# Tap loads of a Fourier convolution: 68 transfers of one tap each in place of 20 transfers of one row group each

## The chip, the cores and the metric

The kernel runs on one core of a Trainium2 chip. The metric is the device time of one execution in microseconds. Three runs of the kernel before are known, and one more execution that was recorded by the hardware profiler.

## What is computed

The input `x` holds 128 graphs of 128 nodes with 256 channels in f32, and `adj` a 128x128 matrix for each graph. Two layers follow one another, each of the form `x = x + layer(relu(layernorm(x)))`. The change touches only the second convolution of the first layer, so that part is shown and the rest is named:

```
h  = relu(bn1(conv1x1(xc)))                  # xc: 256 channels x 128 nodes
h  = bn2(conv1d(h, conv2_w, 17 taps, pad 8))
x_conv = relu(h + xc)
A  = exp(-pairwise squared distance) * adj ; x_nmp = A @ relu(x @ w_msg + b_msg)
out = GRU gates from [x_conv, x_nmp] and x
```

The second layer is a sum of five small graph convolutions over the first 25 nodes of each graph.

## The kernel before, in words

The convolution with 17 taps is done in the Fourier domain. 80 real frequency coefficients are used, and for each of them a 256x256 weight matrix is needed. These matrices are made on the chip from `conv2_w`, whose layout in memory is [256 input channels, 17 taps, 256 output channels].

*Tap weights* (`load_taps`, lines 426 to 433, and `tap_weights`, lines 435 to 474). The 256 input channels are worked off in four groups `n` of 64. One group is loaded into a tile `wt` of 128 partitions x 16 x 256. The 64 channels are four row groups `r` of 16 channels: partitions 32r to 32r+16 hold the 17 taps of row group `r`, and along the free axis lie its 16 channels with 256 outputs each. Two `wt` tiles exist, so group `n+2` can be loaded only when TensorE has read all of group `n`. For each of eight steps `m` TensorE multiplies the 17 rows of each row group by the 17x80 matrix `tap` (four matmuls `pw`, line 450), ScalarE and VectorE copy the four results into a tile `ws` (lines 455 and 457), and after every second step GpSimd issues four stores of 320 KB from `ws` to the tensor `wfd` in memory (line 462). There are two `ws` tiles: the copies of step `m` wait until the stores of step `m-4` have landed. In all 64 stores write 20 MB.

*Stage A* (`stage_a`, lines 367 to 418) runs beside it. For each group `q` of four graphs it loads `xa` with four transfers of 128 KB on SyncE (line 359; four `xa` tiles), takes the layernorm statistics on VectorE (`st`, `mv`, line 267 on), raises the variance to the power -1/2 on GpSimd (`rs`, line 270), normalizes on VectorE (line 275), transposes on TensorE (`ph`, line 386), writes `hTa` by a ReLU on ScalarE (line 388), stores it from GpSimd (`hTd`, line 391), multiplies by `c1w` (`pc`, line 397), adds a row on VectorE (`h`, line 400), and transforms to 80 coefficients (`pf`, line 408) that are copied into `X`. The first 16 of the 32 groups come in the first pass.

*After it*, `early` (line 632) computes the neighbour part of graph groups from reloaded `hT`, and `stage_b` (line 477) multiplies `X` by the weights reloaded from `wfd`. Then the second half of stage A and stage B, and the rest of both layers.

*Order.* Each engine executes its instructions in the order in which the program issues them. That order is written by a small planner (`Lane`, `Order`, lines 156 to 204): each part of the work is a generator whose `yield cost, delay` tells how much TensorE time it has just issued and after how much planned time it may go on. The planner alternates between the lanes by their planned times and weights. The lane `beside` holds `tap_weights` and then `early(0)`, `early(1)` and so on. The first `yield` of `tap_weights`, line 437, sets when the lane starts: after 16 planned microseconds.

*Queues.* Transfers are issued by SyncE, ScalarE and GpSimd, and each of these issues in order: a transfer that has to wait holds up what is behind it. In the compiled program the transfers of SyncE and ScalarE share eight completion semaphores, which are handed out in turn, and those of GpSimd have eight of their own. A transfer that gets a semaphore whose earlier transfer hasn't landed waits for it. Before the tap loads of group 0, ScalarE issues `cst`, `vec` and `c1w`, and SyncE `xa0` and `xa1`. Behind them GpSimd has the powers of `fold` (lines 286 and 270) and ScalarE its first ReLU.

Group 0 of the taps is loaded by the call at line 1103 on three queues. Groups 1, 2 and 3 are loaded from inside `tap_weights` on SyncE and GpSimd (line 441): group 1 at step 3 of group 0, and the others at step 0 of the group before. Behind GpSimd's part stand further `rs` powers, `hTd` stores and `wfd` stores.

Of the kernel before, what the change touches and what calls it, by code (L numbers as in the profile page):

```python
# [16 lines left out]
TAPS, PAD = 17, 8  # L17
# [190 lines left out]
def kernel(ctx: ExitStack, tc: tile.TileContext, x, adj, consts, vecs, w_se, conv1_w,  # L208
                    conv2_w, w_msg, b_msg, w_ih, w_hh, W1, W2, b2, fusion_w, out):
    nc = tc.nc  # L210
# [22 lines left out]
    def c(name):  # L233
        a, b = CAT[name]
        return cst[:, a:b]
# [14 lines left out]
    def load_late():  # L250

        nc.sync.dma_start(out=wse, in_=w_se.rearrange("(k p) o -> p k o", p=P))
        nc.sync.dma_start(out=cst[:, CFIRST:], in_=consts[:, CFIRST:])
# [73 lines left out]
    def fold_embedding():  # L327

        nc.vector.memset(wse9, 0.0)
        for role in range(3):  # L330
            nc.vector.tensor_copy(wse9[:, :, 3 * role:3 * role + 3], wse[:, :, :3])
        pbs = ptmp.tile([P, 512], FP, tag="tmp", name="pbs")
        nc.tensor.matmul(pbs[:, :1], c("sel"), v("b_se"), start=True, stop=True)
        bse = cp.tile([P, 1], FP, name="bse")
        nc.vector.tensor_copy(bse, pbs[:, :1])
        nc.vector.scalar_tensor_tensor(embb, emb[:, 4:8], bse, emb[:, 8:12],
                                       op0=ALU.mult, op1=ALU.add)
        yield 1.5, 0.0
# [23 lines left out]
    def load_xa(q):  # L362
        if q not in XA:
            XA[q] = LATE["ab"].tile([P, 4, D], FP, tag="xa", name=f"xa{q}", bufs=4)
            load_x(XA[q], q)
# [60 lines left out]
    def load_taps(n, *engines):  # L426

        wt = tw.tile([P, 16, D], FP, tag="wt", name=f"wt{n}")
        src = conv2_w.rearrange("(r n i) t o -> n t r i o", r=4, n=4)[n]
        for r in range(4):  # L430
            engines[r % len(engines)].dma_start(out=wt[32 * r:32 * r + 16], in_=src[:16, r])
        engines[0].dma_start(out=wt[16::32], in_=src[16])
        wts.append(wt)

    def tap_weights():

        yield 0.0, 16.0
        for n in range(4):
            for m in range(8):
                if m == (0 if n else 3) and n < 3:  # L440
                    load_taps(n + 1, nc.sync, nc.gpsimd)
                if (n, m) == (1, 3):
                    load_late()
                if m % 2 == 0:
                    ws = tw.tile([P, 4, 4, D], FP, tag="ws", name=f"ws{n}_{m}")
                pws = [(pgat if r < 3 else ptmp).tile([P, 2, D], FP, tag="gat" if r < 3 else "tmp",
                                                      name=f"pw{n}_{m}_{r}") for r in range(4)]
                for r in range(4):
                    rows = slice(32 * r, 32 * r + TAPS)
                    nc.tensor.matmul(pws[r][:F], c("tap")[rows], wts[n][rows, 2 * m:2 * m + 2],  # L450
                                     start=True, stop=True)
                i = m % 2 * 2
                for r in range(4):
                    if r < 2 or (r == 2 and m % 2):
                        nc.scalar.activation(ws[:F, r, i:i + 2], pws[r][:F], AF.Copy)
                    else:
                        nc.vector.tensor_copy(ws[:F, r, i:i + 2], pws[r][:F])
                yield 0.9, 2.2
                if m % 2:
                    for r in range(4):  # L460
                        i0 = 64 * r + 16 * n + 2 * (m - 1)
                        nc.gpsimd.dma_start(out=wfd[:, i0:i0 + 4], in_=ws[:F, r])
        yield from fold_embedding()
        mid.close()
        wg = ctx.enter_context(tc.tile_pool(name="wg", bufs=1, reuse_waits="tile"))
        LATE["wrz"] = wg.tile([P, 7, 3, D], FP, name="wrz")
        LATE["wn"] = wg.tile([P, 7, 2, P], FP, name="wn")
        LATE["wh"] = wg.tile([P, 7, 1, P], FP, name="wh")
        LATE["io"] = near.enter_context(tc.tile_pool(name="io", bufs=2, reuse_waits="tile"))
        LATE["fr"] = near.enter_context(tc.tile_pool(name="fr", bufs=1, reuse_waits="tile"))  # L470
        LATE["wmsg"] = LATE["fr"].tile([P, 2, D], FP, name="wmsg")
        LATE["bmsg"] = LATE["fr"].tile([P, D], FP, name="bmsg")
        nc.sync.dma_start(out=LATE["wmsg"], in_=w_msg.rearrange("(k p) o -> p k o", p=P))
        nc.sync.dma_start(out=LATE["bmsg"], in_=b_msg.partition_broadcast(P))
# [625 lines left out]
    load_xa(0)  # L1100
    nc.scalar.dma_start(out=c1w, in_=conv1_w.rearrange("(k p) o -> p k o", p=P))
    load_xa(1)
    load_taps(0, nc.sync, nc.gpsimd, nc.scalar)
    load_xa(2)
    fold()
    beside = Lane([tap_weights()] + [early(q) for q in range(NQ)])
    gates = Lane([fold_gates()], weight=0.5)
    for bat, (during_a, during_b) in enumerate(((0.66, 0.5), (0.2, 0.65))):
# [60 lines left out]
```

## Time and profile before

| | |
|---|---|
| three runs | 2124.36, 2126.18, 2129.80 us |
| median of the runs | 2126.18 us |
| the profiled execution's own time | 2123.29 us |
| its span, first to last instruction | 2121.2 us |
| mean granted TensorE clock | 0.989 |
| moved by DMA | 281.66 MB, mean 133 GB/s |

The share of busy time on the page is a mean over stages that differ: up to about 212 us the tap weights and stage A run, to about 630 us the first products and the second pass of stage A, and after 700 us the gates and the second layer, in which the DMA engines are busy 30% of the time on the mean. The page's 40 slices are 53 us each:

```
PE   6998999999999999999999999999999999999998
DMA  9997778744787534233223232323222332323121
```

A digit is the busy share of a slice in tenths. In the first three slices DMA and TensorE are both near full. Arrows in a timeline name what ended the idle time before an instruction; "issue" means that the profile shows no waiting. DMA engines are not told apart in the views; a "share" of over 1 comes from packets that overlap on an engine.

### The profile page before, as it was taken

How to read it: one execution, taken by the hardware profiler on the slowest of the kernel's cores; microseconds unless marked ns; L12 is line 12 of the kernel's file. 1: busy time of each engine (PE TensorE's matmuls, PEld its weight loads, DVE VectorE, ACT ScalarE, POOL GpSimd, SP SyncE). 2: the span in 40 equal slices, each digit the busy share in tenths (PEclk: the TensorE clock that was granted, in tenths of full speed). 3: DMA queues.
4: the chain of work that ended last, by engine and by line, in shares of the span. 5: the costliest groups of instructions: out<-in, count | busy, mean ns of one | idle time of the engine just before them, and what ended most of it. 6: DMA issues, size and time to landing. Idle time of an engine off the chain costs nothing.

```text
span 2121.2 us, 30965 instructions
## 1 busy us (share of the span) xinstructions
PE 2056.6 (97%) x11316; PEld 1656.3 (78%) x11316; DVE 1177.2 (55%) x2775; ACT 687.6 (32%) x1543; POOL 723.2 (34%) x900
## 2 busy tenths in 40 slices
PE   6998999999999999999999999999999999999998
PEld 5566888789888787787778777878787787778775
DVE  5665444786544455645654654566455555654542
ACT  3554222344222233332232332232233323223233
POOL 2442666231565123422332233233213323233230
PEclk9999999999999999999999999999999999999999
DMA  9997778744787534233223232323222332323121
GB/s 182 264 269 231 242 267 261 213 145 150 254 267 253 184 110 153 61 100 77 73 71 83 84 83 71 107 73 78 80 82 75 83 97 75 78 80 102 36 68 50
DMA packets 187050, 281.66 MB, mean 133 GB/s; under 512 B 20685, under 2 KB 140242, under 8 KB 186898
## 3 DMA queue, kind: packets, MB, share of 16 engines
q1 hardware_dynamic: 156066, 184.81, 31.2%
q0 software_dynamic: 30000, 94.13, 13.7%
q8 instruction: 90, 1.47, 0.3%
q10 hardware_dynamic: 832, 0.74, 0.2%
q14 instruction: 62, 0.51, 0.1%
HBM read 187.34 MB, written 92.27 MB: 132 GB/s over the span
## 4 chain that ended last, share of the span: by engine, by line
PE 88%; DVE 3%; DMA 3%; POOL 2%; ACT 2%; issue 1%; SPq 0%; POOLq 0%; DVEq 0%; ACTq 0%
PE p L708 39%; PE pa L501 7%; PE pm L600 5%; PE ph L1029 5%; PE pz L1038 5%; PE pc L397 4%; PE pb L501 3%; PE pf L408 3%; PE px L626 3%; PE pi L673 2%; PE pg L1072 1%; DMA wfd<-ws 1%; PE po L853 1%; PE ph L386 1%; PE pw L450 1%
## 5 line engine op out<-in xcount | busy, mean ns | idle before, releaser
L833 POOL TENSOR_TENSOR d<-hTc,r 128x512 f32<-128x512 f32 x64 | 81.4, 1272 | 371.1 <-ACT r L830 371.1
L501 PE MATMUL pa<-wf,X 128*128 128x256 f32 x640 | 152.4, 381 | 0.0
L862 POOL DMA_DIRECT2D out<-xt x128 | 71.8, 566 | 204.2 <-DVE xt L859 201.5
L723 ACT ACTIVATE z<-z,brz 128x256 f32<-128x256 f32 x128 | 58.1, 501 | 253.3 <-DVE z L778 205.6
L524 DVE SCALAR_TENSOR_TENSOR y<-pa,kk 128x512 f32<-128x512 f32 x78 | 53.8, 690 | 147.4 <-ACT kk L523 147.4
L708 PE MATMUL p<-th,wrz 128*128 128x256 f32 x512 | 131.8, 380 | 0.0
L708 PE MATMUL p<-tc,wrz 128*128 128x256 f32 x512 | 131.6, 379 | 0.0
L708 PE MATMUL p<-tm,wrz 128*128 128x256 f32 x512 | 131.4, 379 | 0.0
L501 PEld LDWEIGHTS pa<-wf,X 128*128 128x128 f32 x640 | 118.1, 190 | 16.4 <-issue 2.2
L397 PE MATMUL pc<-c1w,hTa 128*128 128x256 f32 x512 | 124.4, 389 | 3.5 <-ACT ef L588 2.3
L600 PE MATMUL pm<-wmsg,hT 128*128 128x256 f32 x512 | 124.0, 388 | 0.0
L690 DVE SCALAR_TENSOR_TENSOR xc<-pc,s_bn,hTc 128x256 f32<-128x256 f32 x128 | 53.1, 477 | 117.3 <-PE pc L687 117.3
L708 PE MATMUL p<-hTc,wrz 128*128 128x256 f32 x384 | 106.1, 399 | 10.1 <-ACT u L742 10.1
L397 PEld LDWEIGHTS pc<-c1w,hTa 128*128 128x128 f32 x512 | 95.3, 194 | 22.2 <-DVE h L400 4.0
L1029 PE MATMUL ph<-yz,w 128*128 128x96 f32 (+3 forms) x640 | 111.5, 329 | 0.9 <-DVE yz L1014 0.9
L708 PEld LDWEIGHTS p<-hTc,wrz 128*128 128x128 f32 x384 | 68.3, 191 | 55.6 <-ACT u L742 22.5
L600 PEld LDWEIGHTS pm<-wmsg,hT 128*128 128x128 f32 x512 | 97.4, 193 | 16.7 <-issue 1.6
L1031 ACT ACTIVATE hh<-ph,vec 128x96 f32<-128x96 f32 (+3 forms) x160 | 64.3, 403 | 139.8 <-PE ph L1029 130.9
L1038 PE MATMUL pz<-hh,w 128*128 128x96 f32 (+3 forms) x640 | 107.7, 322 | 0.0
L708 PEld LDWEIGHTS p<-tm,wrz 128*128 128x128 f32 x512 | 97.3, 190 | 13.2
L1029 PEld LDWEIGHTS ph<-yz,w 128*128 128x128 f32 x640 | 90.1, 197 | 21.8 <-issue 15.5
L708 PEld LDWEIGHTS p<-th,wrz 128*128 128x128 f32 x512 | 94.5, 190 | 12.6 <-issue 0.6
(203 smaller groups left out, 4590.4 us busy)
## 6 DMA issues: line engine op xcount, KB each, us to landing
wf<-wfd SPq DMA_DIRECT2D x160, 256.0 KB, 3.9
wfd<-ws POOLq DMA_DIRECT2D x64, 320.0 KB, 7.3
yd<-y POOLq DMA_DIRECT2D x80, 256.0 KB, 3.7
yt<-yd SPq DMA_DIRECT2D x64, 320.0 KB, 4.9
w<-in_W SPq DMA_DIRECT2D x40, 512.0 KB, 3.6
xa<-in_x SPq DMA_DIRECT2D x128, 128.0 KB, 5.0
hTd<-hTa POOLq DMA_DIRECT2D x32, 512.0 KB, 5.0
hT<-hTd SPq DMA_DIRECT2D x32, 512.0 KB
```

The source lines that it names most:

```text
L397: nc.tensor.matmul(pc[:, i], hT[:, k, (2 * h + i) * N:(2 * h + i + 1) * N], c1w[:, k], start=(k == 0), stop=(k == 1))
L408: nc.tensor.matmul(pf[:, i, :F * NB], h1[:, 2 * h + i, k * P:(k + 1) * P], fwd, start=True, stop=True)
L501: nc.tensor.matmul(ps, xk(k), WF[f][:, k, s], start=(k == 0), stop=(k == 1))
L600: nc.tensor.matmul(pm[:, i], hT[:, k, j * N:(j + 1) * N], LATE["wmsg"][:, k], start=(k == 0), stop=(k == 1))
L626: nc.tensor.matmul(px[:, dc, i], msgs[h][:, i, dc * P:(dc + 1) * P], aT[:, 2 * h + i], start=True, stop=True)
L708: nc.tensor.matmul(ps[:, m], w[:, i, k, m * P:(m + 1) * P], factor(i, x, t), start=first and j == 0, stop=last and j == len(n) - 1, skip_g ...
L723: nc.scalar.activation(dst[:, m], src[:, m], AF.Sigmoid, bias=brz[:, b + m:b + m + 1])
L833: nc.gpsimd.tensor_sub(d, hT[:, dc], r[:, dc])
L862: nc.gpsimd.dma_start(out=out[q * GB + j, WIDE:].rearrange("(t n) c -> n t c", n=WIDE), in_=xt[j * WIDE:(j + 1) * WIDE, 1:4])
L1029: nc.tensor.matmul(ph, w1[:, k, m * P:(m + 1) * P], yz[:, k, :, o:o + n], start=(k == 0), stop=(k == 1))
L1031: nc.scalar.activation(hh[:, m], ph, AF.Relu, bias=v("b1", g * 4 + m))
L1038: nc.tensor.matmul(pz, w2[:, g, m, cc * P:(cc + 1) * P], hs[g][:, m], start=(m == 0), stop=(m == 3))
```

## The change

Three places differ. In `load_taps` the five transfers of a group (four of 16 taps x 16 channels, 256 KB each, into 16 neighbouring partitions, and one of 64 KB for the 17th tap into partitions 16, 48, 80 and 112) become 17 transfers of 64 KB: transfer `t` takes tap `t` of all 64 channels into partitions t, 32+t, 64+t and 96+t. They go alternately to two queues, the first of which gets nine. For group 0 the queues are GpSimd and ScalarE, no longer SyncE, GpSimd and ScalarE; for the other groups they stay SyncE and GpSimd. And the lane of the tap weights starts after 12 planned microseconds instead of 16.

```diff
         wt = tw.tile([P, 16, D], FP, tag="wt", name=f"wt{n}")
         src = conv2_w.rearrange("(r n i) t o -> n t r i o", r=4, n=4)[n]
-        for r in range(4):
-            engines[r % len(engines)].dma_start(out=wt[32 * r:32 * r + 16], in_=src[:16, r])
-        engines[0].dma_start(out=wt[16::32], in_=src[16])
+        for t in range(TAPS):
+            engines[t % len(engines)].dma_start(out=wt[t::32], in_=src[t])
         wts.append(wt)
 
     def tap_weights():
 
-        yield 0.0, 16.0
+        yield 0.0, 12.0
@@
     load_xa(1)
-    load_taps(0, nc.sync, nc.gpsimd, nc.scalar)
+    load_taps(0, nc.gpsimd, nc.scalar)
     load_xa(2)
```

In the compiled order the number of instructions on TensorE and VectorE stays as it is. From the first `pw` on, the tap work stands about one group of four matmuls and a half tile of stage A further ahead on every engine, and the interleaving of the two lanes stays shifted until well after the first products. SyncE's order becomes `xa0` to `xa4`, nine taps of group 1, `xa5`, `xa6`, nine of group 2, `xa7`, two constants, `xa8` to `xa10`, nine of group 3, `xa11` and so on. Before it was `xa0`, `xa1`, three transfers of group 0, `xa2` to `xa5`, three of group 1, `xa6`, `xa7`, three of group 2, `xa8` and so on.

## The prediction

> **What bounds the kernel now.** I read the page first, then busy time by stretch, the chain of waits from 60 to 200 us, the timelines of the first 36 us, and last the DMA view of single stretches.
>
> ```profile
> span 2121.2 us, 30965 instructions
> PE 2056.6 (97%) x11316; PEld 1656.3 (78%) x11316; DVE 1177.2 (55%) x2775; ACT 687.6 (32%) x1543; POOL 723.2 (34%) x900
> wt<-in_conv_w SPq DMA_DIRECT2D x8, 256.0 KB, 6.5
> wt<-in_conv_w POOLq DMA_DIRECT2D x7, 256.0 KB, 12.2
> ```
>
> TensorE is the bound, 97% busy. The change adds no TensorE work, so it can only move TensorE's 64.6 us of idle time and the stretches at half clock that follow idle time. The tap loads run in the first 130 us, so I looked for loss up to 212 us.
>
> ```profile
> 0.00:36.00 36.00, 18.11 (x84) 15.15 (x88) 16.86 (x63) 6.82 (x12) 6.10 (x11) 0.95 0.96 165
> 36.00:78.00 42.00, 42.00 (x263) 28.48 (x256) 29.82 (x78) 26.34 (x56) 19.28 (x29) 1.00 0.95 233
> 78.00:84.00 6.00, 0.77 (x4) 0.36 (x3) 0.84 (x2) 0.86 (x2) 1.53 (x3) 1.00 1.09 267
> 84.00:113.00 29.00, 29.00 (x159) 18.81 (x158) 21.98 (x59) 16.61 (x36) 13.48 (x20) 0.88 0.93 278
> 172.00:188.00 16.00, 12.05 (x82) 9.63 (x80) 8.26 (x27) 6.95 (x15) 5.44 (x7) 0.95 0.82 246
> ```
>
> The columns after the stretch are its length, busy time of PE, PEld, DVE, ACT and POOL, then granted clock, DMA share and GB/s. The reader is to see one hole, 78 to 84 us, and that the 29 us after it ran at 0.88 of the clock: 5.2 us idle plus 29 x 0.12 = 3.4 us slow, 8.6 us together. Its cause is in the chain:
>
> ```profile
> 68.85 0.90 POOL wfd L462
> 71.68 11.35 DMA wfd<-ws
> 83.14 0.60 ACT ws L455
> 83.78 2.49 PE pw L450 x8
> ```
>
> The second columns are durations. ACT may not fill the next `ws` until GpSimd's store of an earlier one has landed, and that store took 11.35 us where the page's median is 7.3. What the DMA engines did meanwhile:
>
> ```profile
> 56.00:60.00 4.00, 4.00 (x30) 2.76 (x24) 3.63 (x13) 2.60 (x6) 2.32 (x4) 1.00 0.98 386
> 67.00:76.00 9.00, 9.00 (x60) 5.90 (x53) 5.57 (x13) 6.04 (x13) 6.60 (x9) 1.00 1.15 146
> 82.00:86.00 4.00, 2.22 (x8) 0.56 (x8) 2.74 (x9) 1.40 (x3) 0.51 (x1) 0.75 1.04 146
> q1 hardware_dynamic: 1382, 1.31, 115.3%
> ```
>
> The last line is the only queue with packets from 67 to 76 us: SyncE's, with `wt2`, `xa8` and two constants. GpSimd's queue, with five stores issued, moved nothing in 9 us, and all 16 engines together gave 146 GB/s where stores alone got 386. From 82 to 86 us GpSimd's half of `wt2` runs and the rate is 146 again. So a tap load is slow and holds every engine.
>
> The start has the second loss:
>
> ```profile
> 2.14 0.49 ACTq L431 DMA_DIRECT2D wt<-in_conv_w  x1
> 17.02 0.60 ACT L388 ACTIVATE hTa<-ph 128x512 f32<-128x512 f32 x1 [13.08 <-PE ph L386]
> 22.48 0.43 DVE L267 BATCH_NORM_STATS2 st<-xa 128x6 f32<-128x256 f32 x1 [2.88 <-DMA xa<-in_x]
> 25.92 2.25 PE L386 MATMUL ph<-cst,xa 128*128 128x128 f32 x8 [3.83 <-issue]
> ```
>
> VectorE takes the statistics of `xa2` before it normalizes `xa1`. It waited 2.88 us for `xa2`, whose load sits behind 576 KB of taps on SyncE, and TensorE idled 3.83 us; the clock was 0.83 from 20 to 30 us (1.7 us): 5.5 us. The tail of the stage (172 to 212 us) loses 5.3 us idle and about 3.4 us of clock on the loads of `hT`.
>
> **What the Trainium skill says.** "SBUF — State Buffer", section "Door 1: The DMA port swizzle", gives 16 ports for DMA, about 27.2 GB/s each; 16 neighbouring partitions lie on four. That is an estimate of 109 GB/s for one old tap load, and the trace agrees: 130 GB/s from 32 to 36 us, when SyncE's `wt1` fills most of it. "DMA: Bandwidth & Descriptors", section "Why a DMA increments its semaphore by 16 and not by 1", says a transfer uses the largest count of engines up to 16 that divides the slowest dimension of both sides, and from SyncE or ScalarE always the lowest-numbered. Old loads (16 partitions) get 16, new ones (4 partitions) get 4: engines 0 to 3 from SyncE and ScalarE, four in rotation from GpSimd. No view tells engines apart, so the trace doesn't show it. The same page, "Queues, rings and completion order": an engine takes its queues in turn, packet by packet. From 87 to 92 us, with `xa` loads and stores both queued, the mix runs at 410 GB/s, which agrees.
>
> **The change part by part.**
>
> Loads: 20 tap transfers become 68, the bytes (1088 KB a group) stay. No compute instruction is added or removed, only moved. Issues, by the durations before: SyncE 12 to 27 at 0.44 us, ScalarE 1 to 8 at 0.49 us, GpSimd 7 to 33 at 0.59 us.
>
> Start. SyncE issues `xa2` right behind `xa1`; the 576 KB that came between take 5.4 us at 109 GB/s, so `xa2` lands near 17 us and not 22.4. The 2.88 us wait goes. Late next is ScalarE: its eight tap issues stand ahead of its table load and of the ReLU that wrote `hTa0` at 17.02. The compiled order shows what they wait for, since SyncE and ScalarE share eight completion semaphores in turn: `vec`, then `xa0`'s last piece, `xa1`'s last, an own tap, `xa2`'s third and fourth, and for the last one `xa3`'s first. I place that landing at 17 to 20 us: some 2.9 MB lie ahead, at about 155 GB/s (mean of the first 20 us), or faster without the jam. Then 0.5 us issue and 1.28 us table load: ReLU at 19 to 22 us. `pc0` starts 2 to 5 us late, `h1` follows, `xa1` is normalized, and `ph1` comes at 23.7 to 27 us where it was 25.92. I take 2 us gained. Bounds: all 5.5 gained, or 3 lost if `xa3` lands at 24. GpSimd's nine issues end near 6.7 us, 0.7 later for the `s_bn` power, which is not used before 12.83: hidden.
>
> Second group of taps (the hole). The planner's start delay of 12 instead of 16 puts each `pw` ahead of about 2.8 us of stage A on TensorE, so `ws` fills earlier. GpSimd's store of `ws0_6` now stands before the `rs` power that held it until 68.85, and starts near 65. Twelve engines carry no SyncE taps; on the other four a 4 KB store packet (160 ns alone, by the packet records of the trace) takes turns with a 1 KB tap packet (46 ns). Twenty store packets an engine x 206 ns = 4.1 us, with what is queued ahead and 2 us to land: 71 us, before `pw1_2` wants its buffer at 72. The 8.6 us go.
>
> What is late next: (a) GpSimd. Its last four taps wait on semaphores of the `ws0_6` stores, to about 70 us; behind them stand `rs` of `xa6`, `hTd5` and the stores of `ws1_0`. `rs` ends at 72.5 (68.9 before), `ph6` wants its data near 74.5: nothing lost. `ws1_0` lands near 80, wanted at 80.5. (b) SyncE. `xa7` now stands behind all nine taps (before: ahead of them). 9 x 64 packets on 4 engines are 144 packets each: 40 shared at 206 ns and 104 at some 60 ns, 14.5 us from 61.7, then `xa7`'s own 32: it lands at 78 to 83 and VectorE asks near 77. TensorE can run about 3 us ahead. I take 2 us lost. Net gain 6.5 us; bounds 8.6 gained, and 10 lost (rival 3).
>
> Later groups. The third group's hole is small (0.88 and 0.57 us of idle, 1.7 us of clock near 121). I take 1.5 gained, bounds 4 gained and 3 lost.
>
> End of stage A. The last `pw` is 2.9 us earlier, but `pse0` now has 7.8 us of TensorE work between them instead of 9.6 and still waits for `hT0` (9.3 us to land). I take 0.5 gained, bounds 3 either way.
>
> After 212 us only the interleaving differs; its larger gaps (1.34, 1.79, 2.33, 2.89 us) may close or open: 0, bounds 3 either way.
>
> Sum: 2 + 6.5 + 1.5 + 0.5 = 10.5 us off the profiled execution's 2123.29 us (span 2121.2): 2112.8. That execution lies 2.9 below the median of the three runs, 2126.18, so on their scale 2115.7.
>
> **Rivals.**
> 1. Forecast: the jam goes, little comes in its place. 2115.7.
> 2. The hole only changes its owner: GpSimd's waits in (a) and `xa7` in (b) cost TensorE 8 us more than I took. For it: both queues gain entries and in-order waits. Against it: GpSimd idles over half of 36 to 78 us. 2115.7 + 8 = 2124.
> 3. Slower: four engines are too few. If GpSimd's queue always has a packet, each of the 144 tap packets takes 206 ns, 29.7 us; `xa7` lands at 61.7 + 29.7 + 4 = 95 us, 15 us after the last time that does no harm. The hole's 8.6 gained, 15 and 3.4 of slow clock lost is 10 lost; with 4 gained elsewhere, net 6 slower, and with `wt3` treated likewise (4 more) 10: 2136. It decides from about 165 ns a packet on. For it: GpSimd's queue has packets nearly throughout 77 to 97 us (packet records). Against it: stores fill only about half of a 38 us group.
> 4. More: the start and stage A's end lose their holes as well. 3.5 + 2 + 2.5 + 2.5 more: 2105.
>
> That the change doesn't do what it says is excluded by the compiled order, which has the 68 transfers.
>
> **How the numbers follow.** 1: 0.59, 2: 0.21, 3: 0.13, 4: 0.07. Below 0.3% (6.4 us), about what these runs can tell, it is no change. Cases 1 and 4 are faster, 0.66; 2 is the same; 3 slower. The time is case 1's, its own range 2109 to 2121. The whole range takes in 2 and most of 4, and the near edge of 3: 2104 to 2130.
>
> **What would show it.** Right: no hole before `pw1_2`; the stores' median to landing under 7.3 us; the slow 146 GB/s stretches gone; no wait for `xa2` at 22 us. Wrong: ScalarE's first ReLU after 23 us; VectorE waiting on `xa` at 77 us for over 5 us; GpSimd's `rs` held by a tap's wait with TensorE idle behind it. If stores still take 11 us, the ports were not the cause and the forecast falls.

## The result, and the profile after

The changed kernel takes 2163.18 us (median of four runs, 2161.2 to 2165.91), beside 2127.63 us for the kernel before in the same comparison (2124.36 to 2129.8). The ratio is 1.018, with a 95% interval of 1.016 to 1.0199: about 38 us slower, where 10.5 us of gain had been forecast. The range ended at 2130.

First the page of the changed kernel: span, busy time, and the rows of tap loads and stores from the list of DMA issues.

```profile
span 2159.4 us, 31027 instructions
PE 2062.5 (96%) x11316; PEld 1661.8 (77%) x11316; DVE 1185.5 (55%) x2775; ACT 686.8 (32%) x1543; POOL 738.9 (34%) x926
wfd<-ws POOLq DMA_DIRECT2D x64, 320.0 KB, 6.0
wt<-in_conv_w POOLq DMA_DIRECT2D x33, 64.0 KB, 9.4
```

TensorE has the same work and 38 us more of span. The stores land sooner (6.0 us on the median, 7.3 before). But a tap of 64 KB from GpSimd takes 9.4 us, little less than the 12.2 us of the old transfer of 256 KB.

Busy time by stretch of the changed kernel, columns as in the prediction:

```profile
0.00:36.00 36.00, 11.27 (x48) 9.50 (x48) 15.13 (x58) 3.55 (x6) 10.64 (x18) 0.86 0.78 134
36.00:78.00 42.00, 38.40 (x220) 26.24 (x221) 24.75 (x63) 22.85 (x50) 21.88 (x33) 0.96 0.76 207
78.00:99.00 21.00, 17.56 (x103) 11.40 (x100) 8.65 (x22) 9.43 (x21) 7.45 (x13) 1.00 0.96 228
99.00:113.00 14.00, 8.64 (x29) 5.87 (x30) 9.06 (x27) 5.39 (x11) 4.93 (x6) 0.51 0.84 243
201.00:212.00 11.00, 4.27 (x24) 3.27 (x25) 1.25 (x3) 0.91 (x2) 0.00 (x0) 0.54 0.83 279
```

The hole at 78 us is gone. There are three new ones: TensorE is busy 11.3 us of the first 36 (18.1 before), the stretch from 99 to 113 us runs at half clock after a hole, and from 201 to 212 us it is busy for 4.27 of 11 us.

To see where the 38 us come from I summed TensorE's idle time and its busy time multiplied by (1 - granted clock) from the trace, by stretch. Each row is one execution. The us lost:

| stretch (us) | 13-60 | 60-113 | 113-150 | 150-215 | 215-750 | 750-1120 |
|---|---|---|---|---|---|---|
| before | 6.6 | 8.6 | 3.6 | 8.5 | 14.7 | 8.8 |
| changed | 14.7 | 17.0 | 8.9 | 10.9 | 13.9 | 21.8 |
| e2: changed, delay 16 | 14.4 | 12.5 | 6.0 | 6.5 | 21.8 | 8.9 |
| e1: delay 12 alone | 9.1 | 6.8 | 7.5 | 6.4 | 17.4 | 19.9 |
| e12: delay 12, later order as before | 7.3 | 5.3 | 7.5 | 5.1 | 15.3 | 8.9 |
| e13: changed, later order as before | 11.1 | 15.1 | 7.3 | 6.6 | 14.8 | 9.1 |
| e4: first group by taps | 12.3 | 8.5 | 3.8 | 5.3 | 17.3 | 8.8 |
| e8: later groups by taps | 7.9 | 16.7 | 6.7 | 9.5 | 16.3 | 9.0 |
| e14: e8, taps spread | 9.0 | 11.9 | 4.3 | 4.7 | 16.0 | 13.9 |
| e15: wide loads spread | 6.3 | 6.3 | 3.2 | 8.9 | 16.9 | 8.8 |

Changed less before: 8.1 + 8.4 + 5.3 + 2.4 - 0.8 + 13.0 = 36.4 of the 38.2 us between the two spans. 24 us are lost up to 215 us, where the taps are loaded and used, and 13 between 750 and 1120 us, where no tap is in sight. How far single executions scatter shows in two pairs: up to about 170 us e1 and e12 have the same instructions and transfers in the same order, and up to about 190 us so have the changed kernel and e13, yet from 13 to 150 us the rows differ by 3.3 and by 7.1 us.

The start, in the changed kernel's chain of waits from 0 to 30 us (start, duration, what):

```profile
1.19 4.23 DMA vec<-in_vecs
5.42 0.02 issue
5.44 14.31 DMA wt<-in_conv_w
19.75 0.02 issue
19.77 5.64 DMA xa<-in_x
25.41 0.02 issue
25.43 7.98 DMA wt<-in_conv_w
```

and ScalarE's timeline (bracket: idle before, and what ended it):

```profile
2.15 23.81 ACTq L431 DMA_DIRECT2D wt<-in_conv_w  x8
26.00 1.28 ACT L388 ACT_TABLE_LOAD   x1 [26.00 <-DMA wt<-in_conv_w]
27.29 1.08 ACT L388 ACTIVATE hTa<-ph 128x512 f32<-128x512 f32 x2
```

ScalarE spent 24 us on eight issues. Its second tap, issued at 5.44, took 14.31 us to land. SyncE's first piece of `xa3` was given that tap's semaphore, so it was issued at 19.77 and landed at 25.4; ScalarE's eighth tap had the semaphore of that piece. Each queue waited for a transfer of the other. The ReLU that ran at 17.02 came at 27.29.

The longest wait is an earlier one, though. ScalarE's timeline in two smaller windows, with its third and its fourth tap:

```profile
9.73 0.54 ACTq L431 DMA_DIRECT2D wt<-in_conv_w  x1
22.16 0.54 ACTq L431 DMA_DIRECT2D wt<-in_conv_w  x1
```

The fourth tap waited 11.9 us, for the semaphore of `xa1`'s last piece. The other four follow within 3.8 us, and the wait for `xa3` adds only 0.4 us of that. Why `xa1` came so late can be seen in the semaphore records of the traces, which the views don't print. A semaphore is raised in steps: sixteen for a piece of `xa` (128 partitions), five for a tap from SyncE or ScalarE, one soon after its issue and four later. That agrees with the prediction's sixteen and four engines, if a step is an engine's; the steps carry no engine's name. Twelve of the sixteen steps of `xa1`'s last piece had come by 17.6 us, the last four came from 20.8 to 22.1. In the kernel before, the sixteen lie within 1.1 us (13.4 to 14.5).

The second group, in the chain around the old hole and the new one:

```profile
63.83 5.45 DMA wfd<-ws
69.30 0.04 ACTq L454
69.34 0.38 issue
69.72 0.60 ACT ws L454
...
82.76 16.82 DMA xa<-in_x
99.58 0.02 issue
99.59 1.85 DMA xa<-in_x
101.44 0.04 issue
101.48 0.44 DVE st L267
```

with SyncE's timeline:

```profile
72.00 10.13 SPq L431 DMA_DIRECT2D wt<-in_conv_w  x9
82.24 7.28 SPq L359 DMA_DIRECT2D xa<-in_x  x4
```

The store that took 11.35 us takes 5.45. But `xa7` is behind nine taps, is issued from 82.2 us on, and has landed only at 101.4; `pc` waited 8.4 us for what VectorE makes of it, as TensorE's waits from 95 to 112 us show:

```profile
PE pc L397 <- DVE X L414: 8.4, 1, 8.4
```

The semaphore steps have the same pattern as at the start. Of each of `xa7`'s four pieces twelve steps had come by 89.6, 90.5, 91.2 and 94.6 us; the last four came 6.2 to 9.0 us later, from 97.4 to 101.4. In the kernel before, the `xa` pieces issued from 66 to 79 us, behind wide transfers, have at most 1.1 us between the twelfth and the thirteenth step.

### The profile page after: what moved, and what is told of

Same layout as the page of the kernel before. It is cut to its first block, busy times and chain, and to the rows that moved or that the text cites. A ratio compares the mean times of both kernels' runs of the same rounds, so it can differ in the third digit from the quotient of the medians.

```text
span 2159.4 us, 31027 instructions
## 1 busy us (share of the span) xinstructions
PE 2062.5 (96%) x11316; PEld 1661.8 (77%) x11316; DVE 1185.5 (55%) x2775; ACT 686.8 (32%) x1543; POOL 738.9 (34%) x926
## 4 chain that ended last, share of the span: by engine, by line
PE 83%; DMA 6%; POOL 3%; DVE 3%; ACT 2%; issue 1%; SPq 0%; ACTq 0%; POOLq 0%; DVEq 0%
PE p L707 38%; PE pa L500 7%; PE pm L599 5%; PE ph L1028 5%; PE pz L1037 5%; PE pc L397 4%; PE pb L500 3%; PE px L625 3%; PE pi L672 2%; DMA wt<-in_conv_w 2%; PE pf L408 2%; DMA xa<-in_x 2%; PE pg L1071 1%; DMA wfd<-ws 1%; PE po L852 1%
## 5 line engine op out<-in xcount | busy, mean ns | idle before, releaser
L397 PE MATMUL pc<-c1w,hTa 128*128 128x256 f32 x512 | 127.9, 397 | 20.3 <-ACT hTa L388 11.9
L599 PEld LDWEIGHTS pm<-wmsg,hT 128*128 128x128 f32 x512 | 97.1, 192 | 17.3 <-issue 2.4
L1028 PEld LDWEIGHTS ph<-yz,w 128*128 128x128 f32 x640 | 89.0, 195 | 21.7 <-issue 15.8
L707 PEld LDWEIGHTS p<-th,wrz 128*128 128x128 f32 x512 | 95.4, 191 | 12.3 <-PE p L707 0.2
```

What stands on the lines that cost most here:

```text
L397: nc.tensor.matmul(pc[:, i], hT[:, k, (2 * h + i) * N:(2 * h + i + 1) * N], c1w[:, k], start=(k == 0), stop=(k == 1))
L599: nc.tensor.matmul(pm[:, i], hT[:, k, j * N:(j + 1) * N], LATE["wmsg"][:, k], start=(k == 0), stop=(k == 1))
L707: nc.tensor.matmul(ps[:, m], w[:, i, k, m * P:(m + 1) * P], factor(i, x, t), start=first and j == 0, stop=last and j == len(n) - 1, skip_g ...
L1028: nc.tensor.matmul(ph, w1[:, k, m * P:(m + 1) * P], yz[:, k, :, o:o + n], start=(k == 0), stop=(k == 1))
```

## Experiments

Theory at the outset: the loads cost the early 24 us, by waits in order on the queues and on completion semaphores, and the shifted order costs the late 13. Rival D: the delay of 12 costs most of it. Ratios are to the kernel before on the same chip; the excess is (ratio - 1) x 2124 us.

| run | median us | ratio, 95% interval | excess us |
|---|---|---|---|
| e1_delay12 | 2138.92 | 1.0068, 1.0053-1.0083 | 14.4 |
| e2_delay16 | 2142.79 | 1.0090, 1.0073-1.0107 | 19.1 |
| e3_first_wide | 2150.82 | 1.0129, 1.0114-1.0144 | 27.4 |
| e4_first_only | 2129.59 | 1.0022, 1.0013-1.0031 | 4.7 |
| e5_delay12_softmax | 2133.81 | 1.0041, 1.0027-1.0056 | 8.7 |
| e6_first_sync | 2126.57 | 1.0005, 0.9993-1.0018 | 1.1 |
| e7_first_wide2 | 2124.74 | 1.0000, 0.9989-1.0011 | 0.0 |
| e8_later_only | 2140.82 | 1.0076, 1.0059-1.0093 | 16.1 |
| e9_later_sync | 2146.62 | 1.0102, 1.0078-1.0126 | 21.7 |
| e10_later_cut | 2135.34 | 1.0054, 1.0038-1.0070 | 11.5 |
| e11_wide_sync | 2127.47 | 1.0018, 1.0008-1.0028 | 3.8 |
| e12_delay12_pause | 2123.46 | 0.9996, 0.9987-1.0005 | -0.8 |
| e13_after_pause | 2143.38 | 1.0095, 1.0075-1.0115 | 20.2 |
| e14_taps_spread | 2128.90 | 1.0024, 1.0015-1.0033 | 5.1 |
| e15_wide_spread | 2118.23 | 0.9968, 0.9955-0.9980 | -6.8 |

### The parts alone

The kernel before with the delay alone (e1), and the changed kernel with the delay undone (e2):

```diff
-        yield 0.0, 16.0
+        yield 0.0, 12.0
```

> The kernel before with only the planner's start delay of 12 instead of 16 (the tap loads stay wide). Idle time and slow clock of TensorE put the loss of 38 us in two places: 24 us up to 215 us, and 13 us between 750 and 1120 us, where no tap is loaded any more. Theory L (the loads do it): the early part belongs to the tap transfers and only the late 13 us can come from the shifted order, so this run is 0 to 14 us slower than before, about 2134, with an undisturbed first 60 us. Rival D (the delay does it): the earlier start of the tap products takes TensorE's turn while stage A is still short of data, and this run is over 25 us slower.

> The kernel after with the start delay put back to 16, all taps still tap by tap. Theory L: the early 24 us stay, the late 13 us go: about 2150. Rival D: over 25 of the 38 us go, 2138 or less.

e1 landed at the upper edge of theory L (14.4 us). e2 lies between the two values that had been named (2150 and 2138): undoing the delay takes 19 of the 38 us off. The delay alone doesn't do what rival D says, since its first 215 us lose only 2.5 us more than the kernel before. But it costs 14 us.

The first group as before in the changed kernel (e3), and the first group alone changed in the kernel before (e4), core of the edit:

```diff
+        if n == 0:
+            for t in range(TAPS):
+                engines[t % len(engines)].dma_start(out=wt[t::32], in_=src[t])
...
-    load_taps(0, nc.sync, nc.gpsimd, nc.scalar)
+    load_taps(0, nc.gpsimd, nc.scalar)
```

> The kernel after, but the first group of taps loaded as before (five wide transfers on three queues). Theory S (ScalarE's tap issues hold its first ReLU until a piece of xa3 has landed): hTa0 is written near 17 us again, the first 60 us lose some 20 us and not 28, and the time is 8 to 10 us below the kernel after, about 2154. Rival: the start only moves the loss (the second group's taps then start earlier into the same xa loads), and less than 4 us are gained.

> The kernel before, but the first group of taps loaded tap by tap on the queues of GpSimd and ScalarE; delay 16, later groups wide. Theory S: ReLU at about 28 us, TensorE idle 11 us ahead of its first pc, 8 to 10 us slower than before: about 2136. Rival (the hole at 78 us has slack that takes the delay in, since its taps are then late by as much): less than 4 us slower.

e3 is 11 us below the changed kernel. e4 has the hole in full (ReLU at 27.41, 10.5 us of idle time ahead of `pc`), but loses 4.7 us and not 8 to 10: by the table 5.7 us at the start and 3.2 us given back from 150 to 215 us. The later groups alone (delay 16, first group wide):

> The kernel before with the later three groups tap by tap on SyncE and GpSimd, first group wide, delay 16. If the parts add up, this is the 18 us of all taps less the 4.9 of the first group: 13 slower, about 2138. Theory W (a tap takes 6 to 11 us to land, and the queue's next entries wait for that landing in order): TensorE waits near 65 to 75, 97 to 106 and 136 to 145 us for stores that GpSimd could issue only when a tap had landed. Rival: without the late start of the first group the second group's taps have time to land, and the loss is under 6 us.

16.1 us: a little more than the sum had left for it, and e4 + e8 = 20.8 agrees with e2's 19.1. The holes are where theory W had them. The chain of e8 to its first new hole:

```profile
53.51 6.76 DMA wt<-in_conv_w
60.27 0.02 issue
60.29 0.02 POOLq L466
60.31 0.47 issue
60.77 0.01 POOLq L270
60.79 7.24 DMA wfd<-ws
...
68.84 0.04 issue
68.89 1.13 PE pw L454
```

GpSimd issued eight taps from 50.9 to 56.7 us, one on each of its semaphores. Five stores stood behind them; the last of the four from `ws` had the semaphore of a tap that landed at 60.27, was issued at 60.79, and the `ws` that `pw` needed came free at 68. But theory W has only part of the cause. GpSimd's timeline, the kernel before first:

```profile
49.60 1.20 POOL L431 DMA_DIRECT2D wt<-in_conv_w  x2
50.94 5.74 POOL L436 DMA_DIRECT2D wt<-in_conv_w  x8
```

The first store from `ws` was issued at 58.65 and not at 51.36. Of these 7.3 us the eight issues themselves are 4.5 (5.74 less 1.20); the waits for taps to land are 1.4 us ahead of the stores and 0.6 us more between them. At 84 us (9.54 us for the tap) and 123 us (11.68 us) chains of the same kind stand again. In the row that begins at 77.6 us GpSimd waited 4.1 us for earlier stores ahead of its last taps, and 4.3 us for taps ahead of the next stores.

### The late 13 us: the order, not the lateness

In e1 TensorE is short between 842 and 860 us. The waits view of TensorE there, then VectorE's timeline:

```profile
PE p L708 <- DVE r L815: 1.9, 1, 1.9
PE p L708 <- DVE v L809: 1.5, 1, 1.5
PE p L708 <- DVE r L823: 1.5, 1, 1.5
```

```profile
845.57 0.15 DVE L893 TENSOR_REDUCE fmx<-fus 128x1 f32<-128x5 f32 x1
845.76 0.23 DVE L894 TENSOR_SCALAR fus<-fus,fmx 128x5 f32<-128x5 f32 x1
847.82 0.16 DVE L897 TENSOR_REDUCE fsm<-fus 128x1 f32<-128x5 f32 x1 [1.83 <-ACT fus L895]
```

The softmax of `fusion_w`, five numbers, stands on VectorE ahead of the gate work `r`, `tm` and `v` on which TensorE waits, and it waits 1.83 us for ScalarE's Exp. After that gap TensorE runs at half clock from 854 to 868 us. The kernel before has the same instructions at 850.6 to 854.3 us, behind `xc`:

```profile
852.81 0.16 DVE L897 TENSOR_REDUCE fsm<-fus 128x1 f32<-128x5 f32 x1 [1.42 <-ACT fus L895]
```

There the wait for the Exp is 1.42 us, and TensorE has some twenty gate matmuls to run meanwhile: its longest idle time there is 0.32 us. Moving the softmax by a planner delay (e5), and restoring the whole later order (e12, e13):

```diff
+        yield 0.0, 12.0
         fmx = pool.tile([P, 1], FP, name="fmx")
```

```diff
+        yield 0.0, 3.0
         yield from fold_embedding()
```

> The kernel before with the start delay of 12, and with one further planner delay of 12 put ahead of the small softmax of fusion_w in setup_1. In the run with the delay alone, 10.6 of its 14 us were lost between 750 and 870 us, where that softmax (a ScalarE Exp with a table load, and a row of small VectorE operations) stands ahead of VectorE's r and tm, for which TensorE waits. With the further delay the Exp stands behind xc again, as in the kernel before. Theory O (the order of this chain costs it): about 10 us come back, 2128. Rival: the loss has other causes (each new order finds its own holes), and the run stays at 2135 or above.

> The kernel before with the start delay of 12, and a planner delay of 3 put behind the last pw, ahead of fold_embedding. With it the instructions of every engine stand in the order of the kernel before from about 180 us on; up to there the order is that of delay 12. Theory O (what the delay costs comes from the later order alone): the 14 us go but for the 2 to 3 that the windows show up to 215 us: 2124 to 2128. Rival D: the early shift costs it, 2135 or above.

> The changed kernel with the same planner delay of 3 ahead of fold_embedding, so that its order from about 180 us on is that of the kernel before. Theory O: 13 us come back, about 2150, and what stays (24 us up to 215 us) is the loads'. Rival: the late 13 us come from being late itself, not from the order, and the time stays above 2158.

e5: the loss from 750 to 870 us fell from 12.3 to 2.4 us, but 870 to 1000 us lost 3.2 us more than in the kernel before, and the total fell by 5.7 us only: half of the theory, and half of the rival. e12 settles it: with the early part at delay 12 and the later order as before, all 14 us are gone. In the changed kernel the same pause takes 18 us off (e13), more than the 13 expected. From 750 to 1120 us the later order costs 11.0 us (e1 less e12) and 12.7 us (changed less e13). The further difference between 14 and 18 can't be laid on the order: by the table, the rows of the second pair differ by 7.1 us up to 150 us, where the order is the same. By 215 us e13 has lost 12.8 us more than the kernel before, and from there to 1120 us only 0.4 more. So being late costs nothing there by itself; what cost it is the interleaving that the planner's clock happened to give. It doesn't hold for every run: e2 has the order of the kernel before on all four computing engines and loses 7.1 us more between 215 and 750 us; why isn't shown.

### The start: who issues the taps

e6 leaves the first group tap by tap, but gives ScalarE's eight to SyncE, behind `xa2`. e7 leaves it wide and takes only the choice of queues from the change.

```diff
-    load_taps(0, nc.sync, nc.gpsimd, nc.scalar)
     load_xa(2)
+    load_taps(0, nc.gpsimd, nc.sync)
```

> The kernel before with the first group tap by tap as in the changed one, but ScalarE's eight taps issued by SyncE instead, behind xa2, which is moved ahead of them. Same transfers, same four partitions each. Theory S (ScalarE is held as the issuer of transfers): ReLU near 17 us again, no idle time of 10 us ahead of pc, and the 4.9 us of the run with only the first group by taps come back: 2122 to 2126. Rival N (the narrow transfers crowd the engines, and xa1 and xa2 land late by that): TensorE waits as long, now for xa1 or xa2, and the time stays near 2130.

> The kernel before with the first group still in five wide transfers, but on GpSimd and ScalarE alone (the choice of queues without the taps). xa2 is no longer behind taps on SyncE. ScalarE issues two taps instead of one, the second after vec has landed (about 5 us), so it is free well before 17 us. What the prediction hoped for at the start, 2 to 5.5 us of the wait for xa2, should show here: 2120 to 2124. Rival: the wide transfers occupy all engines and xa2 lands no earlier, the same time as before.

e6 is as fast as the kernel before. ScalarE's timeline in e6:

```profile
2.14 1.28 ACT L388 ACT_TABLE_LOAD   x1 [2.14 <-issue]
16.70 0.60 ACT L388 ACTIVATE hTa<-ph 128x512 f32<-128x512 f32 x1 [13.28 <-PE ph L386]
```

Same transfers, same partitions, and the ReLU is back at 16.70: it was late because ScalarE issued taps. How long ScalarE had to wait is in part the shape's, by the four late steps of `xa1`; e6 doesn't separate that, since its eight taps are also issued behind `xa2`. The gain hoped for isn't there either: TensorE idles 4.2 us ahead of `ph1` (3.8 before). In e7 that wait shrank to 2.2 us, but the first matmul came at 16.29 us and not at 14.05 (up to 15.6 in the other runs with the old start), since VectorE could begin on `xa0` only at 12.72 and not at 10.49 (11.99 in e14, with the old start). The three wide transfers on GpSimd beside it are a likely reason, not a shown one. Nothing is left of the gain. The Trainium skill, "DMA: Bandwidth & Descriptors", section "Issuing engines are not separate DMA queues", says that spreading DMAs over several issuers saves only the issuing time, since all run on the same 16 engines. e7 agrees with that; the changed kernel shows that it can also cost, where the issuer has computing to do.

### The later groups: burst, count or shape

All 17 taps on SyncE (e9), and the wide transfers cut in four along `i`, so that the count is 17 and the shape is 16 partitions (e10):

```diff
-                    load_taps(n + 1, nc.sync, nc.gpsimd)
+                    load_taps(n + 1, nc.sync)
```

```diff
+                for i in range(0, 16, 4):
+                    engines[r % len(engines)].dma_start(out=wt[32 * r:32 * r + 16, i:i + 4],
+                                                        in_=src[:16, r, i:i + 4])
```

> As the run with only the later groups tap by tap (16.5 us slower than before), but all 17 taps of a group on SyncE; GpSimd issues none. Theory W (eight taps on GpSimd hold all eight of its completion semaphores, so that each of the next stores is issued only when a tap has landed): the three holes ahead of pw near 69, 102 and 143 us go, and 10 us or more come back: 2124 to 2130. Rival N (the narrow transfers crowd four engines whoever issues them): SyncE needs over 20 us for 17 taps, xa8 and xa11 come late, TensorE waits for VectorE's statistics instead: 2136 or above.

> The kernel before, with each wide tap transfer of the later groups cut into four along i: 17 transfers a group as in the tap-by-tap version, on the same two queues, but each to 16 neighbouring partitions. Theory W (the count on GpSimd decides): the same holes as with the taps, 2136 to 2141. Rival N (the four-partition shape decides): as before, 2122 to 2128.

e9 takes away the hole at 69 us (one of 3.3 us stands at 83) and still gets slower. SyncE's timeline in e9 shows why:

```profile
65.63 20.63 SPq L436 DMA_DIRECT2D wt<-in_conv_w  x17
86.37 5.05 SPq L359 DMA_DIRECT2D xa<-in_x  x4
```

17 issues took 20.6 us, and `xa` behind them landed at 100.6, TensorE waiting 7.0 us near 106 and 5.8 us near 147. While stores ran beside, from 78 to 86 us, SyncE's queue moved 177 packets; on four engines that is 181 ns each. The first two `xa` pieces behind the taps have twelve steps by 89.2 and 90.0 us and the last four from 94.4 and 94.7 on. So W was wrong to say that freeing GpSimd would do, and N describes e9. In e10 the count alone, without the narrow shape, costs 11.5 us, and there no `xa` piece issued from 73 to 88 us has more than 0.4 us between its twelfth and thirteenth step. What the shape adds in a burst is thus about 4.6 us (e8 less e10), but the intervals of the two ratios overlap.

That leaves the burst. e14 issues the taps of e8 three or four at a time between the `pw` steps, e15 the kernel before's wide transfers one or two at a time, and e11 puts the wide ones on SyncE alone. In e14 and e15 TensorE, VectorE and ScalarE keep the order of the kernel before, instruction by instruction.

```diff
-                    load_taps(n + 1, nc.sync, nc.gpsimd)
+                    loading = load_taps(n + 1, nc.sync, nc.gpsimd)
+                for _ in range(1 if n else 2):
+                    next(loading, None)
```

(`load_taps` yields after each transfer; e14 has `3 if n else 4`.)

> As the run with only the later groups tap by tap on SyncE and GpSimd (16.5 us slower), but a group's 17 transfers are issued three at a time (four in the first group) between the pw steps, and not in one burst. The order on TensorE, VectorE and ScalarE is that of the kernel before. Theory B (the burst: eight taps in a row on GpSimd's in-order queue and nine ahead of xa on SyncE's): no store and no xa load waits behind more than two taps, and at least 10 of the 16.5 us come back, 2124 to 2131. Rival N (a tap to four partitions is slow beside the stores whenever it is issued): the holes stay, spread over the group, 2136 or above.

> The kernel before with its wide tap transfers issued one or two at a time between the pw steps, order of the three computing engines unchanged. If theory B is right it holds for the wide burst as well, whose hole at 84 us cost the kernel before 8.6 us: 2116 to 2121, faster than both kernels. Rival: one wide transfer alone is enough to hold the stores, and the time is that of before.

> The kernel before with the wide transfers of the later groups all on SyncE. If GpSimd's own tap transfers in front of its stores were the cost, the hole at 84 us shrinks by its part from 82 to 86 us: 2119 to 2123. Rival N: SyncE's queue then holds the stores for 11 us instead of 7 and xa comes later: 2126 or above.

e14 gives back 11 of e8's 16 us with shape, count and queues unchanged: the burst is the larger part. At most 5 us stay with the narrow taps; its hole of 4.2 us near 72 us is one where `pw` waits for a tap itself, which took 7.12 us. (5.1 us of its loss lie between 870 and 1000 us, as slow clock at the order of the kernel before, and can't be laid on the taps.) e15 beats both kernels, 6.8 us below the kernel before. The old hole in e15:

```profile
36.00:78.00 42.00, 42.00 (x261) 28.31 (x262) 30.06 (x79) 26.59 (x56) 19.27 (x30) 1.00 0.90 243
78.00:84.00 6.00, 3.14 (x13) 1.03 (x11) 2.74 (x9) 1.40 (x3) 0.95 (x2) 0.84 1.04 336
84.00:113.00 29.00, 29.00 (x171) 19.96 (x168) 21.94 (x60) 17.91 (x38) 13.38 (x20) 0.92 0.91 256
```

It is half as deep (3.14 us busy of six, 0.77 before), and by the table 60 to 113 us lose 6.3 us where they lost 8.6. That accounts for the 2.3 us between the two profiled spans (2118.9 and 2121.2), not for the whole 6.8 of the timed runs; where the rest lies isn't shown (the profiled execution, 2121.05 us, is the slowest of e15's six). e11 moved the hole to 86 us and kept its depth (5.9 us idle): it followed its rival in direction and costs 3.8 us.

## Why the prediction was wrong, point by point

- **The bound and the mechanism** were read rightly as far as they go. The old hole is gone in the changed kernel, its stores land in 6.0 us, and the store that took 11.35 takes 5.45. The 146 GB/s stretch is not wholly gone: from 84 to 92 us the mean is 190. Two readings said too much. The first of the five stores was issued only at 68.85 us and the fifth at 73.91, so GpSimd's queue had work standing for 7.2 of the 9 us (its next packet is at 76.05). And if the engines had taken the queues in turn there, with store packets ready, some would have moved; none did, and why isn't shown. The 410 GB/s of a mixed stretch shows that both queues move, not that they take turns.
- **Start**, forecast 2 gained, bounds 5.5 gained to 3 lost: 8.1 lost in the changed kernel, 4.7 as a part alone. The failed step is the landing of the pieces that ScalarE waits for, placed from bytes over bandwidth: `xa3`'s first at 17 to 20 us. Measured 25.4. The bandwidth taken was 155 GB/s; the first 25.4 us ran at 133. The chain of semaphores was named correctly, but taken as a place in a stream, and not followed back once more: the piece itself could be issued only when ScalarE's own tap had landed, 14.31 us after its issue. And the last link was not the one that mattered: `xa1`'s last piece, at 22.1, already holds the ReLU to about 26.9 (my estimate, 27.29 less the 0.4 us of the last wait). The four crowded engines that rival 3 counts for the second group were not counted here. The ReLU's limit that I set for being wrong, 23 us, was passed by 4. Also wrong: that `xa2` moves forward. Its last piece landed at 24.4 and not at 22.3, and VectorE could begin on `xa1` at 22.3 where it did at 17.2.
- **Second group**, forecast 6.5 gained: 8.4 lost. The old hole's 8.6 went, but in part by luck: the store had landed at 69.28 and SyncE's taps were issued only from 72.0 on, so the two never met. Where they did, in e9, a hole of 3.3 us stands at 83. What failed is step (b). `xa7` was put at 78 to 83 us and landed at 101.4. That is the place and the size of rival 3 (95 us, 10 lost), and its four engines show in the late last four steps of each piece. Its rate does not: the taps were issued from 72.0 and not from 61.7, after a start that was itself late, and their packets took about 98 ns on four engines (244 from 78 to 84 us), not 206. In e9, with nothing but taps on the queue, the 181 ns come near it. Step (a), that GpSimd's taps hold nothing that matters, failed too: in e8 its stores went out 7.3 us late behind them.
- **Later groups and the end of stage A**, forecast 2 gained: 7.7 lost. From 113 to 150 us it is of the same kind, `pw` waiting 4.4 and 1.3 us for `ws`. At the end of the stage `pse` waited 8.2 us for `hT` (3.1 before, 5.9 in e8, none in e13), so loads and order both move that wait.
- **After 212 us**, taken as 0 with 3 either way: 12.2 lost, by e12 and e13 nearly all of it the planner's order (0.7 and 0.4 us stay). This is the largest single term, and it was not worked out at all. The compiled order was at hand and showed that the interleaving stays shifted; the bound of 3 was taken from the size of the gaps that existed, which says nothing of gaps that a new order opens.

Of the 38 us, 20 are the loads (20.2 in e13, 19.1 in e2), 4.7 of it from the first group and 16.1 from the later ones (e4, e8). Taking the shifted order away takes 18 off, of which 13 can be placed between 750 and 1120 us. What is open: whether the 14 us of the shift in the kernel before and the 18 in the changed one differ by more than scatter, and how much of e14's 5 us is the narrow shape. The semaphore steps give the count of engines for SyncE's and ScalarE's taps, not which ones; GpSimd's taps have sixteen steps each, so for them not even the count is shown.

## What to carry to other kernels

Count transfers before bytes: a row of issues takes the issuer's time and every completion semaphore of its queue, and what comes next may have to wait for one of them to land, so spread loads between the steps that use the queue, and follow each wait on a semaphore back to the transfer that held it before. An engine with work on the critical path should issue no transfer that must wait. After any edit of a planner's costs or delays, read the order behind it as well, or hold it fixed: 14 us came with one `yield` here and went with another.

## What the runs showed of the hardware that was not expected

- A 64 KB load to four partitions lands 9.4 us after GpSimd's issue on the median, where 256 KB to 16 partitions takes 12.2: a quarter of the bytes for three quarters of the time. Both times include the waiting in the row.
- A load to all 128 partitions is as late as its last steps: behind taps to four partitions, twelve of its sixteen completion steps came 6.2 to 9.0 us ahead of the last four (`xa7` in the changed kernel), behind transfers to 16 partitions at most 1.1 us.
- An issue can take much longer than its usual 0.5 us: three of SyncE's tap issues in e9 are recorded with 2.2, 3.6 and 2.7 us, at 76 to 84 us, towards the end of a row of 17.
- ScalarE's table load took 1.28 us, as the Trainium skill has it ("ScalarE: Activation LUTs", section "What ACT_TABLE_LOAD costs"), and in front of a softmax of five numbers that is 1.28 of the 1.83 us that VectorE waited in e1.
